# Issue order, piece sizes and the place of an addition in a quantised gated feed-forward kernel: gate casts in halves, gate tiles behind evacuations, two pieces in the first units of down, x1 by VectorE

## The chip, the cores and the metric

One core of one Trainium2 chip. The metric is the device time of one execution in microseconds (us). The engines carry the profile's names: PE (TensorE, matmuls), DVE (VectorE), ACT (ScalarE), POOL (GpSimd) and SP (SyncE, which here issues DMAs). Each engine takes its instructions one after the other in the order in which they were issued to it; an instruction that waits holds up what is behind it on its engine, which the timelines of this kernel show as idle time with a releaser.

## The reference

Two layers on x of 2 x 2048 tokens by 512. The first adds a cross attention to a context of 2 x 128 rows. The second is the one that matters here:

```python
# act_qdq(x): one scale for the whole tensor, x rounded to 16 bit integers
# lpbq_dequant(w): one scale for each block of 32, w rounded to 4 bits
x = act_qdq(x)                                # x: layernorm of layer 1's sum
up = act_qdq(x @ lpbq_dequant(w_up).T)        # 512 -> 1536
gate = act_qdq(x @ lpbq_dequant(w_gate).T)    # 512 -> 1536
sig = fixed_qdq_u16(jax.nn.sigmoid(gate))
gate = act_qdq(gate * sig)
o = act_qdq(gate * up)
return o @ lpbq_dequant(w_down).T             # 1536 -> 512, added to layer 1's sum
```

Each act_qdq needs the maximum over the whole tensor before its first element can be rounded. So the stages gate, up and down follow each other, and what one stage produces is kept or goes through HBM.

## The kernel before

**Exact integers on PE.** The integers of an operand are split into three parts (the integer divided by a base and rounded, in the code `sa`, which ACT casts to part 0; the rest, part 1; and a combination, part 2). A product is then two sums in PSUM: q, over parts 0 and 1, and e, over part 2. ACT *evacuates* q, that is, copies it from PSUM scaled, and DVE then joins e to it.

**Stages** in the profiled execution: attention, layernorm and the weights of gate up to 157 us; gate, 158 to 434; up, 435 to 700; the scale of the product, 700 to 711.5; down, 711.5 to 978.

**Gate** (L683 to L720). Eight token groups of 512, in each three tiles of four chunks: 96 chunks, numbered 0 to 95. A chunk is 12 matmuls (8 for q, 4 for e, 2.72 us on PE). ACT evacuates its q (L712), DVE subtracts e and notes the maximum (L713). q and e have three PSUM buffers each. `split_integers` (L251 to L254) makes the parts of the next token group: sa on DVE, its cast on ACT, parts 1 and 2 on DVE, each over 128 x 2048. Between the chunks a generator advances the preparation of the weights of up and down: eight batches, each with DVE steps over 128 x 1536 (L197 to L213), 12 transposes on PE in three groups (L205, two PSUM buffers) and three copies on ACT (L206).

**Up** (L873 to L900). 48 half tiles c of 24 matmuls (5.44 us). ACT evacuates q (`u`, L876) from two PSUM buffers; DVE subtracts e (L877); ACT takes the absolute value (L817), DVE the maximum of the product with the kept gate values (L818). For each of 24 gate tiles, loaded by SP one and two ahead (`gt`), ACT makes the integers (gi, L769), the sigmoid (L770) and its 16 bit value (sq, L771), each over 128 x 2048; DVE multiplies them to p (L810). `next_gelu` issues the three ACT instructions after a half tile's evacuation in the code, and the scheduler may set them before it. `parts_u` (L750) are the parts of a token group, loaded by SP from HBM.

**The scale of the product** (L905 to L944). While DVE, POOL and ACT find it, PE runs matmuls that nobody reads (`idle`, L912): five behind the transpose of the maxima, one later.

**Down** (L1017 to L1200). 32 units m, one for 128 tokens: 24 matmuls of q (L1032, `yq`) and 12 of e (L1040, `ye`), 8.16 us on PE. A unit's integers o come from p and u: DVE `oi` = p x k_o x u (L1017), DVE `sa` (L1018), ACT cast to part 0 (L1021), DVE part 1 (L1020), DVE part 2 (the "third", L1024). The 1536 inner elements are 12 blocks of 128. Unit 0 takes them in pieces of 2, 2, 4 and 4 blocks, the units 1 to 4 in three pieces of 4, all later ones in one piece of 12. For m = 0 to 3 p is read from the three kept tiles of 4 blocks (`kept_p`); from m = 4 on from one loaded tile (`p5`). The parts have two buffers, by m. ACT also rounds u to integers (`ui`, L995) for the next units.

An output m is finished while unit m + 2 is prepared: ACT evacuates q (`yqs`, L1045), POOL adds x1, which is layer 1's sum (`qx`, L1047), DVE adds the scaled e (L1051) and SP stores it (L1053). The evacuation of m - 2 stands on ACT ahead of the first cast of m. `in_order` (L169) fixes the order in which instructions are issued without a wait; what it does not fix, a scheduler decides.

## Time and profile before

| | us |
|---|---|
| median of 3 runs | 983.13 |
| lowest, highest | 981.88, 984.56 |
| the profiled execution | 983.28 |
| its span in the profile | 981.5 |
| PE busy | 946.1 |
| DVE busy | 816.8 |
| ACT busy | 549.5 |
| POOL busy | 87.1 |

The span begins with the first instruction and ends with the last; the execution's own time is 1.8 us longer. The profile is of one execution. A row of a timeline gives the start, the duration, the engine, the line of the code, the operation, what it writes and reads with shapes, a count when several like rows follow each other, and in brackets how long the engine had stood idle before it and which instruction let it go. Instructions of one engine overlap a little at their ends, so costs that add up are taken from start to start.

### The profile page before, as it was taken

How to read it: one execution, taken by the hardware profiler on the slowest of the kernel's cores; microseconds unless marked ns; L12 is line 12 of the kernel's file. 1: busy time of each engine (PE TensorE's matmuls, PEld its weight loads, DVE VectorE, ACT ScalarE, POOL GpSimd, SP SyncE). 2: the span in 40 equal slices, each digit the busy share in tenths (PEclk: the TensorE clock that was granted, in tenths of full speed). 3: DMA queues.
4: the chain of work that ended last, by engine and by line, in shares of the span. 5: the costliest groups of instructions: out<-in, count | busy, mean ns of one | idle time of the engine just before them, and what ended most of it. 6: DMA issues, size and time to landing. Idle time of an engine off the chain costs nothing. (4 is left out here: it accounts for less than half of the span.)

```text
span 981.5 us, 11779 instructions
## 1 busy us (share of the span) xinstructions
PE 946.1 (96%) x4352; PEld 763.1 (78%) x4352; DVE 816.8 (83%) x1007; ACT 549.5 (56%) x665; POOL 87.1 (9%) x66
## 2 busy tenths in 40 slices
PE   6998889999999999999999999999899999999998
PEld 6775656888878888877888888877587888888886
DVE  4979878898998898447988888969799999998782
ACT  3477699323233323229999999895445355453531
POOL 0101110000000000000000000000111332222221
PEclk9999999999999999999999999999999999999999
DMA  9675546976995954896997979979783686656710
GB/s 358 244 283 200 186 166 262 410 303 243 383 359 182 344 195 170 282 410 244 373 323 290 406 284 368 379 264 407 294 326 117 222 268 234 203 177 227 263 62 36
DMA packets 103596, 263.72 MB, mean 269 GB/s; under 512 B 6064, under 2 KB 46000, under 8 KB 94832
## 3 DMA queue, kind: packets, MB, share of 16 engines
q1 hardware_dynamic: 102496, 259.02, 71.4%
q0 software_dynamic: 512, 2.88, 0.8%
q10 hardware_dynamic: 528, 1.05, 0.3%
q8 instruction: 34, 0.56, 0.2%
q14 instruction: 26, 0.21, 0.1%
HBM read 136.05 MB, written 126.88 MB: 268 GB/s over the span
## 5 line engine op out<-in xcount | busy, mean ns | idle before, releaser
L621 PE MATMUL q_g<-parts_g,wg 128*128 128x512 f32 x768 | 192.7, 392 | 2.1 <-ACT g L712 1.2
L621 PEld LDWEIGHTS q_g<-parts_g,wg 128*128 128x128 f32 x768 | 143.1, 188 | 32.6 <-ACT parts_g L644 2.0
L712 ACT ACTIVATE g<-q_g 128x512 f32<-128x512 f32 x96 | 57.2, 599 | 168.3 <-PE q_g L621 157.6
L621 PE MATMUL q_u<-parts_u,wu 128*128 128x512 f32 x576 | 142.5, 389 | 1.8 <-ACT u L876 1.2
L621 PEld LDWEIGHTS q_u<-parts_u,wu 128*128 128x128 f32 x576 | 108.0, 188 | 24.9 <-ACT u L876 2.6
L1032 PE MATMUL yq<-wd,o_parts 128*128 128x512 f32 x512 | 121.6, 389 | 0.5 <-ACT o_parts L1021 0.5
L1032 PEld LDWEIGHTS yq<-wd,o_parts 128*128 128x128 f32 x512 | 96.0, 188 | 21.0 <-ACT o_parts L1021 0.9
L627 PE MATMUL e_g<-parts_g,wg 128*128 128x512 f32 x384 | 103.3, 390 | 0.0
L713 DVE CUSTOM_DVE_ANT_0 g<-g,e_g 128x512 f32<-128x512 f32 x96 | 64.4, 679 | 40.1 <-PE e_g L627 36.8
L1021 ACT CAST o_parts<-sa 128x1536 fp32r<-128x1536 int16 (+2 forms) x43 | 49.1, 1145 | 67.9 <-DVE sa L1018 67.7
L627 PEld LDWEIGHTS e_g<-parts_g,wg 128*128 128x128 f32 x384 | 71.8, 188 | 15.2 <-DVE gtop L713 0.3
L1047 POOL TENSOR_TENSOR qx<-yqs,x 128x512 f32<-128x512 f32 x32 | 63.1, 1973 | 205.2 <-ACT yqs L1045 147.0
L627 PE MATMUL e_u<-parts_u,wu 128*128 128x512 f32 x288 | 77.0, 389 | 0.0
L1024 DVE SCALAR_TENSOR_TENSOR o_parts<-sa,oi 128x1536 fp32r<-128x1536 int16 (+2 forms) x43 | 62.5, 1475 | 10.9 <-PE ye L1040 10.9
L877 DVE TENSOR_TENSOR u<-u,e_u 128x1024 f32<-128x1024 f32 x47 | 56.8, 1217 | 16.6 <-ACT u L876 16.5
L1032 PE MATMUL yq<-first_wd,o_parts 128*128 128x512 f32 x256 | 65.2, 398 | 3.7 <-ACTq L1090 2.1
L1045 ACT ACTIVATE yqs<-yq,q_o 128x512 f32<-128x512 f32 x32 | 21.9, 684 | 80.3 <-PE yq L1032 80.2
L818 DVE CUSTOM_DVE_ANT_0 ua<-ua,pi 128x1024 f32<-128x1024 f32 x46 | 56.0, 1219 | 12.9 <-ACT ua L817 12.8
L1020 DVE SCALAR_TENSOR_TENSOR o_parts<-sa,oi 128x1536 fp32r<-128x1536 int16 (+2 forms) x43 | 59.0, 1372 | 8.3 <-PE yq L1032 5.3
L1040 PE MATMUL ye<-wd,o_parts 128*128 128x512 f32 x256 | 63.2, 389 | 0.0
L627 PEld LDWEIGHTS e_u<-parts_u,wu 128*128 128x128 f32 x288 | 54.1, 188 | 11.2
L1032 PEld LDWEIGHTS yq<-first_wd,o_parts 128*128 128x128 f32 x256 | 48.9, 192 | 15.7 <-ACTq L1090 2.9
(213 smaller groups left out, 1571.6 us busy)
## 6 DMA issues: line engine op xcount, KB each, us to landing
gate_d<-g SPq DMA_DIRECT2D x24, 1024.0 KB, 7.7
up_d<-u SPq DMA_DIRECT2D x48, 512.0 KB, 8.8
gt<-gate_d SPq DMA_DIRECT2D x22, 1024.0 KB, 8.3
u<-up_d SPq DMA_DIRECT2D x21, 1024.0 KB, 9.0
parts_d<-parts_g SPq DMA_DIRECT2D x6, 3072.0 KB, 12.3
parts_u<-parts_d SPq DMA_DIRECT2D x6, 3072.0 KB, 15.6
p_d<-pi SPq DMA_DIRECT2D x24, 512.0 KB, 9.9
p<-p_d SPq DMA_DIRECT2D x84, 128.0 KB, 2.8
```

Of the source, the lines that this page charges most:

```text
L621: nc.tensor.matmul(q, lhsT=w[:, s, c, :], rhs=parts[:, s, c, :], start=(c + s == 0), stop=(c + s == ND))
L627: made = nc.tensor.matmul(e, lhsT=w[:, 2, c, :], rhs=parts[:, 2, c, :], start=(c == 0), stop=(c == ND - 1))
L712: evacuated = nc.scalar.activation(g4[:, i, :], q, AF.Copy, scale=1.0 + 1.0 / BASE)
L713: subtracted = nc.vector.tensor_tensor_reduce(g4[:, i, :], g4[:, i, :], e, 1.0, LOWEST, ALU.subtract, ALU.max, gtop[:, m : m + 1])
L818: nc.vector.tensor_tensor_reduce(ua, ua, pi, 1.0, 0.0, ALU.mult, ALU.max, pumax[:, c : c + 1])
L877: less = nc.vector.tensor_tensor(u4[:, both, :], u4[:, both, :], e, ALU.subtract)
L1020: made.append(nc.vector.scalar_tensor_tensor(parts[1][:, c], sa[:, c], -BASE, oi[:, c], ALU.mult, ALU.add))
L1021: return made, nc.scalar.copy(parts[0][:, c], sa[:, c])
L1024: return nc.vector.scalar_tensor_tensor(parts[2][:, c], sa[:, c], BASE + 1.0, oi[:, c], ALU.mult, ALU.subtract)
L1032: nc.tensor.matmul(q, lhsT=parts[s][:, f, :], rhs=wd[f][:, s, :], start=(f + s == 0), stop=(f + s == NF))
L1040: nc.tensor.matmul(e, lhsT=parts[2][:, f, :], rhs=wd[f][:, 2, :], start=(f == 0), stop=(f == NF - 1))
L1047: nc.gpsimd.tensor_tensor(qx, qs, x1[:, m % NU, :], ALU.add)
```

## The change

Four edits, in the order of the diff.

1. Gate: from token group 1 on, `split_integers` works in two halves of 128 x 1024 (sa, cast, parts 1 and 2 of the first half, then of the second). The scheduler then orders much of gate's DVE and ACT work anew.
2. Up: from half tile 4 on, the first of the three ACT instructions of a gate tile may not be issued ahead of the evacuation of that half tile.
3. The scale of the product: six and two idle matmuls for five and one.
4. Down: the units 1 to 4 take their blocks in two pieces, 4 and 8; in the units 1 to 3 the piece of 8 reads p with two instructions of 4, since p lies in two tiles. Part 2 is one instruction of 12 (in unit 0, one of 4 and one of 8). The outputs 0 to 3 have no POOL addition: ACT evacuates to `qs`, DVE adds the scaled e into it and then adds x1 in an instruction of its own, and the store reads `qs`, which has two buffers. In unit 0 the small operations of the output's scale stand behind part 2. The three round-ups of u that are issued with unit 3 stood one behind each cast; now one stands behind the first cast and two behind the second.

```diff
@@ -683,7 +683,7 @@
                 if t == 0:
                     parts = first
                 else:
-                    parts = split_integers(wk1, homes[t % 2], hi[t], [ND, TG], f"g{t}")
+                    parts = split_integers(wk1, homes[t % 2], hi[t], [ND, TG], f"g{t}", 2)
                 if t < NG - 2:
                     nc.sync.dma_start(out=parts_d[t], in_=parts.bitcast(F32))
                 else:
@@ -762,11 +762,13 @@
         s_g16 = const.tile([P, 1], F32, name="s_g16")
         nc.vector.tensor_scalar(s_g16, s_g, 1.0 / 65536.0, None, ALU.mult)
 
-        def gelu_like(pool, gt, shape, name):
+        def gelu_like(pool, gt, shape, name, behind=None):
 
             sq = pool.tile([P] + shape, U16, tag="sq", name=f"sq_{name}")
             gi = pool.tile([P] + shape, I16, tag="gi", name=f"gi_{name}")
-            nc.scalar.activation(gi, gt, AF.Copy, scale=r_g)
+            begun = nc.scalar.activation(gi, gt, AF.Copy, scale=r_g)
+            if behind is not None:
+                in_order(behind, begun)
             nc.scalar.activation(gt, gi, AF.Sigmoid, scale=s_g)
             nc.scalar.activation(sq, gt, AF.Copy, scale=65536.0)
             return gi, sq
@@ -792,11 +794,11 @@
 
         wd, ready, made_p = [], [], []
 
-        def next_gelu():
+        def next_gelu(behind):
 
             j = len(ready)
             if j < len(order):
-                ready.append(gelu_like(wk3, gts.pop(0), [NQ, TG], j))
+                ready.append(gelu_like(wk3, gts.pop(0), [NQ, TG], j, behind))
                 if j + 2 < len(order):
                     gts.append(load_gate(j + 2))
 
@@ -873,7 +875,7 @@
                     e = ps_m.tile([P, 2, TG], F32, tag="e", name=f"e_u{c}")
                     for i in range(2):
                         project(wu2[i], parts, q[:, i, :], e[:, i, :])
-                    nc.scalar.activation(u4[:, both, :], q, AF.Copy, scale=1.0 + 1.0 / BASE)
+                    evacuated = nc.scalar.activation(u4[:, both, :], q, AF.Copy, scale=1.0 + 1.0 / BASE)
                     less = nc.vector.tensor_tensor(u4[:, both, :], u4[:, both, :], e, ALU.subtract)
                     if c + 2 == NH:
                         in_order(row_known, less)
@@ -890,7 +892,8 @@
                     load_down(range(NE, NE + NQ), slice(0, 2))
                 stored = nc.sync.dma_start(out=up_d[c], in_=u4[:, both, :])
                 if h == 0 or c in more_gelu:
-                    next_gelu()
+
+                    next_gelu(evacuated if c > 3 else None)
                 if h == 0 or c in more_p:
                     next_p()
                 pi = kept_p[j % NK]
@@ -918,7 +921,7 @@
 
 
         a_u, turned = over_partitions_by_pe(ps_m, "q", [P, 2, TG], umax, "u")
-        in_order(before[-1], turned, *(behind := idle(5, u4[:, 0, :])))
+        in_order(before[-1], turned, *(behind := idle(6, u4[:, 0, :])))
 
         r_u = const.tile([P, 1], F32, name="r_u")
         nc.vector.tensor_scalar(r_u, a_u, 1.0 / QMAX, tiny_u, ALU.mult, ALU.max)
@@ -939,7 +942,7 @@
             if i == 0:
                 nc.vector.tensor_scalar(most[:, 3:4], best[:, 1:2], r_u, 1.0 + 2.0**-18, ALU.mult, ALU.mult)
                 nc.vector.tensor_scalar(most[:, 3:4], most[:, 3:4], 0.5 * (QMAX + 2.0), None, ALU.add)
-        in_order(behind[-1], *idle(1, product[:, :TG]))
+        in_order(behind[-1], *idle(2, product[:, :TG]))
         top = const.tile([P, 4], F32, name="top")
         nc.gpsimd.partition_all_reduce(top, most, P, bass_isa.ReduceOp.max)
 
@@ -1011,10 +1014,15 @@
         ]
         oi, sa = (wki.tile([P, NF, P], I16, tag=tag, bufs=1, name=tag) for tag in ("oi", "sa"))
 
-        def round_o(parts, pi, ui, c=slice(None)):
-
+        def round_o(parts, pis, ui, c=slice(0, NF)):
+
+            n = (c.stop - c.start) // len(pis)
             made = [
-                nc.vector.scalar_tensor_tensor(oi[:, c], pi, k_o, ui, ALU.mult, ALU.mult),
+                nc.vector.scalar_tensor_tensor(
+                    oi[:, ds(c.start + i * n, n)], pi, k_o, ui[:, ts(i, n)], ALU.mult, ALU.mult
+                )
+                for i, pi in enumerate(pis)
+            ] + [
                 nc.vector.tensor_scalar(sa[:, c], oi[:, c], 1.0 / BASE, None, ALU.mult),
             ]
             made.append(nc.vector.scalar_tensor_tensor(parts[1][:, c], sa[:, c], -BASE, oi[:, c], ALU.mult, ALU.add))
@@ -1043,6 +1051,8 @@
         def finish_first(m, q, x1):
             qs = wk2.tile([P, D], F32, tag="qs", name=f"yqs_{m}")
             made = nc.scalar.activation(qs, q, AF.Copy, scale=q_o)
+            if m < NS * NU:
+                return made, qs
             qx = wk2.tile([P, D], F32, tag="qx", name=f"qx_{m}")
             nc.gpsimd.tensor_tensor(qx, qs, x1[:, m % NU, :], ALU.add)
             return made, qx
@@ -1050,6 +1060,9 @@
         def finish(m, qx, e):
             made = nc.vector.scalar_tensor_tensor(qx, e, e_o, qx, ALU.mult, ALU.add)
             t = m // NU
+            if m < NS * NU:
+
+                nc.vector.tensor_tensor(qx, qx, x1s[t][:, m % NU, :], ALU.add)
             nc.sync.dma_start(out=of[ds(groups[t // NS] * TG + t % NS * TD + m % NU * P, P), :], in_=qx)
             return made
 
@@ -1068,10 +1081,11 @@
             nc.vector.reciprocal(k_o, k_o)
 
         def scale_of_o():
-            nc.vector.tensor_tensor(s_o, a_o, s_pu, ALU.mult)
+            begun = nc.vector.tensor_tensor(s_o, a_o, s_pu, ALU.mult)
             nc.vector.tensor_scalar(s_o, s_o, 1.0 / QMAX, TINY, ALU.mult, ALU.max)
             nc.vector.tensor_scalar(q_o, s_o, BASE + 1.0, None, ALU.mult)
             nc.vector.tensor_scalar(e_o, s_o, -BASE, None, ALU.mult)
+            return begun
 
         uis = {0: up_integers(0)}
         a_o = const.tile([P, 1], F32, name="a_o")
@@ -1084,7 +1098,7 @@
         factor_of_o()
 
 
-        first_made, first_cast = round_o(o_parts[0], kept_p[0][:, :2, :P], uis[0][:, :2, :P], slice(0, 2))
+        first_made, first_cast = round_o(o_parts[0], [kept_p[0][:, :2, :P]], uis[0][:, :2, :P], slice(0, 2))
         in_order(*first_made)
         known = nc.values_load(flag[0:1, 0:1], min_val=0, max_val=1)
         with tc.If(known == 0):
@@ -1136,7 +1150,7 @@
                     nc.vector.tensor_copy(kept_p[k], pv)
                 scale_of_pu()
                 factor_of_o()
-                in_order(*round_o(o_parts[0], kept_p[0][:, :2, :P], uis[0][:, :2, :P], slice(0, 2))[0])
+                in_order(*round_o(o_parts[0], [kept_p[0][:, :2, :P]], uis[0][:, :2, :P], slice(0, 2))[0])
 
         ld = c5.enter_context(tc.tile_pool(name="ld", bufs=2))
         last = NT // TD - 1
@@ -1156,43 +1170,41 @@
                 if j == NU - 1 and t < last:
                     x1s[t + 1] = load_x1(t + 1)
                 ui, w, parts = uis[t], ts(j, P), o_parts[m % 2]
-                if t < NS or m == NS * NU:
-
-                    casts, made = [], []
-                    sizes = [2, 2, NQ, NQ] if m == 0 else [NQ] * NK
-                    pieces = [slice(sum(sizes[:i]), sum(sizes[: i + 1])) for i in range(len(sizes))]
-                    for n, c in enumerate(pieces):
-                        if m == n == 0:
-                            continue
+
+                sizes = {0: [2, 2, NQ, NQ], NS * NU: [NQ, 2 * NQ]}.get(m, [NQ, 2 * NQ] if t < NS else [NF])
+                pieces = [slice(sum(sizes[:i]), sum(sizes[: i + 1])) for i in range(len(sizes))]
+                casts, made = [], []
+                for n, c in enumerate(pieces):
+                    if m == n == 0:
+                        continue
+                    if t < NS:
                         k, i = divmod(c.start, NQ)
-                        if t < NS:
-                            v = kept_p[k][:, ds(i, c.stop - c.start), ds(t * TD + j * P, P)]
+                        at = ds(t * TD + j * P, P)
+                        if c.stop - c.start > NQ:
+                            v = [kept_p[k + d][:, :, at] for d in range((c.stop - c.start) // NQ)]
                         else:
-                            v = p5[t][:, c, w]
-                        done, cast = round_o(parts, v, ui[:, c, w], c)
-                        made += done
-                        casts.append(cast)
-                    made += [third_part(parts, c) for c in pieces]
-                    in_order(*made)
+                            v = [kept_p[k][:, ds(i, c.stop - c.start), at]]
+                    else:
+                        v = [p5[t][:, c, w]]
+                    done, cast = round_o(parts, v, ui[:, c, w], c)
+                    made += done
+                    casts.append(cast)
+                if m == 0:
+                    made += [third_part(parts, slice(0, NQ)), third_part(parts, slice(NQ, NF))]
                 else:
-                    made, cast = round_o(parts, p5[t][:, :, w], ui[:, :, w])
-                    casts = [cast]
                     made.append(third_part(parts))
-                    in_order(*made)
+                in_order(*made)
                 if m > 1:
                     in_order(evacuated, casts[0])
                 sums[m] = first_sum(m, parts), second_sum(m, parts)
                 if m == 0:
-                    scale_of_o()
+                    in_order(made[-1], scale_of_o())
                     in_order(casts[-1], *round_up(ui, 0, P, P))
                 if j == (0 if t == 0 else NU - 1) and t < last:
                     uis[t + 1] = up_integers(t + 1)
                     rounded = round_up(uis[t + 1], t + 1)
                     if t == NS - 1:
-                        for cast, done in zip(casts, rounded):
-                            in_order(cast, done)
-                        in_order(rounded[0], casts[1])
-                        in_order(rounded[1], casts[2])
+                        in_order(casts[0], rounded[0], casts[1], *rounded[1:])
                     else:
                         in_order(casts[-1], *rounded)
                     if t % NS == NS - 2 and t + NS <= last:
```

## The prediction

> **What bounds the kernel now.** The page's first section gives PE 96% of the span, so only PE's waits can be won. I read the table of PE's waits first, for those near the edited lines; then the timelines of the engines that end them; then the order in which the changed program issues its instructions on each engine. Four are near the edits (columns: engine, line, who released it: us in total, times, longest):

> ```profile
> PE q_u L621 <- ACT u L876: 2.6, 2, 1.3
> PE yq L1032 <- ACT o_parts L1021: 2.2, 2, 1.6
> PE yq L1032 <- ACTq L1090: 2.1, 1, 2.1
> ...
> PE q_g L621 <- ACT g L712: 1.2, 1, 1.2
> ```

> With smaller ones PE idles 12.9 us after 150 us. That is all there is to win behind the preparation.

> **Down's first units.** The timeline from 743 to 757 shows what L1032 waits for. First PE, then DVE, then POOL (start, duration, what it does, in brackets idle time and releaser):

> ```profile
> 750.43 2.11 PE L1032 MATMUL yq<-wd,o_parts 128*128 128x512 f32 x8 [0.53 <-ACT o_parts L1021]
> ...
> 756.89 0.50 PE L1032 MATMUL yq<-first_wd,o_parts 128*128 128x512 f32 x1 [1.64 <-ACT o_parts L1021]
> ```

> ```profile
> 747.57 0.75 DVE L1017 SCALAR_TENSOR_TENSOR oi<-p,k_o,ui 128x512 int16<-128x512 int16 x1
> 748.35 1.32 DVE L1018 TENSOR_SCALAR sa<-oi 128x512 int16<-128x512 int16 x1
> 749.78 0.69 DVE L1020 SCALAR_TENSOR_TENSOR o_parts<-sa,oi 128x512 fp32r<-128x512 int16 x1
> 750.39 1.89 DVE L1024 SCALAR_TENSOR_TENSOR o_parts<-sa,oi 128x512 fp32r<-128x512 int16 x3
> 752.20 0.74 DVE L1051 SCALAR_TENSOR_TENSOR qx<-ye,e_o,qx 128x512 f32<-128x512 f32 x1
> 752.86 1.81 DVE L1017 SCALAR_TENSOR_TENSOR oi<-p,k_o,ui 128x1536 int16<-128x1536 int16 x1
> 754.77 0.56 DVE L1018 TENSOR_SCALAR sa<-oi 128x1536 int16<-128x1536 int16 x1
> ```

> ```profile
> 748.23 1.29 POOL L1047 TENSOR_TENSOR qx<-yqs,x 128x512 f32<-128x512 f32 x1 [6.57 <-ACT yqs L1045]
> ```

> DVE has no idle time from 711.4 to 757: here it is the bound, and PE follows it through the cast. The sa row of 1.32 us begins while POOL's add runs; the same shape takes 0.29 at 719 to 747 us where POOL is quiet. The four adds of outputs 0 to 3 meet sa at 728.59 (1.19) and 748.35 (1.32) and the thirds at 722.97 (2.98) and 740.42 (3.00, against 1.89): 0.90 + 1.03 + 1.09 + 1.11 = 4.1 us of DVE.

> What one unit costs on DVE: a 4-wide piece is oi, sa, p1, start to start 0.78 + 0.33 + 0.61 = 1.72 (up to 1.8 further on), three of them 5.3; thirds 1.81; finish 0.66; in all 7.8, and with an add 8.9. PE's unit is 8.16 (729.79 to 737.96).

> After: a 4-wide piece stays 1.72. The 8-wide one has two oi (0.66 + 0.78), one sa and one p1 over 1024, which the trace lacks: by the 512 and the 1536 rows sa lies from 0.33 to 0.67, p1 from 0.61 to 1.76 (start to start); I take the middles, 0.50 and 1.19, since 1024 lies in the middle: piece 3.13. The third over 1536 is 1.76. Sum 6.61. A finish is 0.66 plus the new add of x1, taken as 0.61 (512-wide rows start 0.60 to 0.66 apart); x1 lies there, since POOL reads it at these times now. Unit: 7.88, with nothing on POOL until m = 4's add. So DVE falls under PE's 8.16.

> Walk: m = 0 is unchanged up to 715.95, its thirds end 717.75. m = 1 is done at 724.4, m = 2 at 731.0, finish 0 at 732.2, m = 3 at 738.9, finish 1 at 740.1, m = 4 at 746.7, finish 2 at 748.0. Then m = 5 as before: from oi's start to PE's start 756.89 - 752.86 = 4.03, so 752.0. PE needs it at 729.79 + 3 x 8.16 = 754.3, or 2.3 us later. PE's start of m = 1 at 721.50 stays: it is set by ACT, whose cast at 720.84 stands behind six round-ups of 5.07 us. **Gain: 756.89 - 754.27 = 2.6 us**; with sa and p1 at their upper ends, 0.74 more in each of four units, 3.0 in all, the slack goes and 0.7 with it: 1.9. More than 2.6 is not to be had, since PE then is the bound. The idle time of 0.53 + 1.64, with overlap lost at both, says the same.

> What is new: the outputs 0 to 3 are stored from qs, two buffers, so the evacuation of y2 waits for the store of y0, y3's for y1's. Behind it on ACT stand the first cast of m = 4 and of m = 5. Stores land after 2.0 us (median 2.8, one of 11.1). Finish 0 ends at 732.2; with 0.3 for the issue, y2's buffer is free at 734.5 to 743.6, and m = 4's cast is due at 745.5. For y3: 742.4 to 751.5, its evacuation of 0.68, and m = 5's cast of 1.47 has to start at 752.8. I cost it at nothing; were each store the slowest, 0.6 us of cover would be left. The 3 DMA issues of these outputs on SP come no later than before.

> [...]

> **Idle matmuls**, one more at two places. One takes 0.43 per pass, 0.86 in all (L912: 10 passes, 4.46). They fill PE gaps of 1.28 (ends 708.35) and 2.08 (ends 711.55), whose ends other engines set: 707.93 and 710.4 are earlier. Cost 0; if they ran at half clock, 0.3. The granted clock is 0.5 from 711.29 to 714.70, so that down's first 8 matmuls take 3.55 instead of 1.98. If busier PE avoids this, PE waits for m = 1's cast at 721.5 all the same: gain 0 to 0.2, and 1.0 if ACT's round-ups were not last. I take 0.

> **Gate.** PE's stall at 270.5 is read from ACT:

> ```profile
> 268.29 1.91 ACT L252 CAST parts_g<-sa_g 128x2048 fp32r<-128x2048 int16 x1 [7.13 <-DVE sa_g L251]
> 270.11 1.06 ACT L206 COPY wsp_u<-wt_u 128x512 f32<-128x512 f32 x2
> 271.43 0.58 ACT L206 COPY wsp_u<-wt_u 128x512 f32<-128x512 f32 x1 [0.26 <-PE wt_u L205]
> 271.91 1.59 ACT L712 ACTIVATE g<-q_g 128x512 f32<-128x512 f32 x3
> ```

> ACT stood 7.13 us at a cast whose sa DVE made late (267.54, behind weight steps and a maximum); three evacuations queued behind it, and PE lost 0.24 + 1.17 us and its overlap, some 0.16. In the changed order the halves of this sa stand on DVE behind chunk 33's subtraction, and the casts on ACT behind evacuation 35, with the weight's transposes later: the cast finds its input ready, the stall of 1.6 goes. What is late next: the transposes of a weight batch, which use two PSUM buffers; adding row by row, six of the eight batches have their third group wait 0.23, against two such waits before (0.24 in that stall, 0.26 at 354.6). Net 1.2, bounds 0 and 1.6.

> Price of the halves: start to start 2.21 over 2048 and 0.61 over 512 give 1.14 over 1024, so 0.08 more for each of 3 x 7 operations, 1.6 us of DVE and as little on ACT (1.91 against two of 1.0). DVE is 105 of 113 us busy in this stage and runs behind PE by up to two chunks, which three PSUM buffers cover. One spot is tight: the second half of token group 2's third part stands behind chunk 23's subtraction and is needed 2.3 us after chunk 24 begins (10 matmuls of 0.227); subtraction 0.69 and half 1.14 leave 0.4. If DVE is a weight step late there (1.75), PE waits 1.3.

> [...]

> **Up.** The gelu tile's gi moves behind the evacuation. Up to evacuation 9 ACT's order is the same, so the 1.34 at 462.70 stays. The other 1.23 is at the end:

> ```profile
> 658.44 2.00 ACT L769 ACTIVATE gi<-gt,r_g 128x2048 int16<-128x2048 f32 x1 [0.24 <-DMA gt<-gate_d]
> 660.35 1.00 ACT L876 ACTIVATE u<-q_u 128x1024 f32<-128x1024 f32 x1
> 661.26 2.00 ACT L770 ACTIVATE gt<-gi,s_g 128x2048 f32<-128x2048 int16 x1
> ```

> After, gate tile 20's gi starts 2.8 us earlier (633.0), but evacuations 36 to 39 now stand behind the sigmoid, 1.9 later in the order. Walk: u36 637.8, u37 645.3, u38 653.8 to 655.0, u39 ends 661.4 to 662.6 (before 661.26), the spread from the load of the next gate tile, which SP issues when the tile two back is done and which lands 7.2 to 8.8 us later. Cost -0.1 to +1.3. But the same load, moved 2.7 us up, lets SP issue the load of parts_u earlier, and PE's 0.52 us wait for it at 667 goes. Net -0.5 to +0.8; I take 0.

> **Sum.** 2.6 + 0 + 1.2 + 0 = 3.8 off the profiled execution's 983.28 (span 981.5 and 1.8 around it; 0.15 over the median of three, 983.13): **979.4 us**.

> **Rivals.** What a measurement can tell from no change is about 0.3%, 2.95 us, so "faster" means under 980.2.
> - *Forecast*, 0.48: 978.3 to 980.6; under 980.2 in 0.42 of it.
> - *Down's gain alone*, 0.27: gate's tight spot (1.3) and up's tail (0.8) take back what gate gives: 983.28 - 2.6 - 1.2 + 2.1 = 981.6; with either, 980.3 to 981.0. For it: DVE at 93% in gate.
> - *More*, 0.13: all of gate's 1.6, up's 0.5, and up to 1.0 from the clock: 983.28 - 2.6 - 3.1 = 977.6, down to 976.5.
> - *Down doesn't do what it says*, 0.06: the long sa and thirds came from the loads and stores of these units and not from POOL, and stay: 4.1 later, and half of the 3.0 above: 757.6, no gain but 0.7 lost; with gate 983.28 + 0.7 - 1.2 = 982.8. Against: all four stand beside an add.
> - *Slower*, 0.06: in gate DVE falls a whole weight step behind at each of the six boundaries between token groups 1 to 7, so a half comes 1.2 late at each: +7.2 - 2.6 = 987.9. At group 2 it decides from a DVE backlog of 0.4; against it: at the other boundaries the halves stand three or more chunks of 2.72 ahead, and a backlog of 8 us would be needed.

> So faster 0.42 + 0.13 = 0.55, same 0.06 + 0.27 + 0.06 = 0.39, slower 0.06. The range 976.5 to 983.0 leaves out the last case and the noise of the runs (981.88 to 984.56) above it.

> **What would show it.** Down: PE without a wait on L1021, m = 5 at 754.3 less the earlier gains; sa never over 0.6. Gate: no wait of PE for g L712, its end 1.2 earlier. Up: 1.3 at evacuation 3 as before, and 1.2 to 2.5 near half tile 41. Wrong would be PE waiting for casts of the gate, stores that hold up yqs, or a stall that moves from L1021 to L1045.

## The result, and the profile after

The changed kernel takes 980.62 us, the median of 20 executions (978.43 to 984.71), against 983.58 for 20 of the kernel before (980.76 to 985.75): a ratio on record of 0.9975, with a 95% interval of 0.9966 to 0.9984 (the two medians alone give 0.9970). That is a gain of 0.25%, clear of noise and less than the 0.4% of the forecast. The profiled execution of the changed kernel took 981.48, its span is 979.7.

The two spans differ by 1.8 us only, and they may not be compared as they stand. Cut by PE's own marks, which are the first matmul of each stage:

| stretch (us) | before | after | difference | forecast |
|---|---|---|---|---|
| start to gate's first q_g | 158.29 | 159.49 | +1.20 | 0 |
| gate, to up's first q_u | 276.92 | 275.38 | -1.54 | -1.2 |
| up, to the transposes of the maxima | 267.27 | 268.01 | +0.74 | 0 |
| scale, to unit 0 of down | 9.07 | 9.07 | 0 | 0 |
| down, unit 0 to unit 5 | 45.34 | 43.07 | -2.27 | -2.6 |
| unit 5 to the end | 224.60 | 224.69 | +0.09 | 0 |

The first row has nothing to do with the change. The granted clock shows 0.5 for one window of 3.413 us in the preparation before, and for two after. Over all 14 profiled executions of this study the first q_g came at 156.5 to 156.8 in four without such a window, at 158.2 to 158.6 in seven with one in the profile's records of that stretch, and at 158.2 to 159.9 in three with two. Single executions of one kernel lie 5 to 6 us apart, and these windows go with some 3 of it (the first q_g at 156.5 to 159.9). Without that row the change is worth 2.98 us in this pair of profiles, inside the interval of the timed runs (0.9966 to 0.9984 of 983.6 is 1.6 to 3.3 us). So the stretches are the finer measure, and the experiments are read by them.

The table of PE's waits after, cut to the lines that answer to those of before (in L621 the line of ACT is now L878, in down L1029 stands for L1021, L1104 for L1090):

```profile
PE q_u L621 <- ACT u L878: 3.5, 3, 1.7
...
PE yq L1040 <- ACT o_parts L1029: 1.2, 3, 0.5
...
PE yq L1040 <- ACTq L1104: 1.2, 1, 1.2
```

Gate's wait for g is gone from the table. Up has three waits and 3.5 us where it had two and 2.6. Down still waits for casts, but three times for little: these are in the units 0 and 1, and none is in unit 4 or 5. PE's timeline after, at unit 5, shows no idle time where there were 1.64 us:

```profile
753.20 1.98 PE L1048 MATMUL ye<-wd,o_parts 128*128 128x512 f32 x8
755.02 1.98 PE L1040 MATMUL yq<-first_wd,o_parts 128*128 128x512 f32 x8
```

DVE's timeline after, for one unit (m = 3), which is to be read against the unit of before:

```profile
733.79 0.29 DVE L1026 TENSOR_SCALAR sa<-oi 128x512 int16<-128x512 int16 x1
734.19 0.69 DVE L1028 SCALAR_TENSOR_TENSOR o_parts<-sa,oi 128x512 fp32r<-128x512 int16 x1
734.80 1.41 DVE L1021 SCALAR_TENSOR_TENSOR oi<-pi,k_o,ui 128x512 int16<-128x512 int16 x2
736.31 0.43 DVE L1026 TENSOR_SCALAR sa<-oi 128x1024 int16<-128x1024 int16 x1
736.85 1.22 DVE L1028 SCALAR_TENSOR_TENSOR o_parts<-sa,oi 128x1024 fp32r<-128x1024 int16 x1
738.00 1.75 DVE L1032 SCALAR_TENSOR_TENSOR o_parts<-sa,oi 128x1536 fp32r<-128x1536 int16 x1
739.66 0.75 DVE L1061 SCALAR_TENSOR_TENSOR yqs<-ye,e_o,yqs 128x512 f32<-128x512 f32 x1
```

From start to start: sa over 1024 costs 0.54 here (forecast 0.50), p1 1.15 (1.19), part 2 over 1536 1.66 (1.76), and no sa is stretched.

And ACT's timeline after, around gate's old stall:

```profile
261.70 0.60 ACT L712 ACTIVATE g<-q_g 128x512 f32<-128x512 f32 x1 [2.12 <-PE q_g L621]
262.60 2.00 ACT L252 CAST parts_g<-sa_g 128x1024 fp32r<-128x1024 int16 x2 [0.31 <-PE e_g L627]
264.51 0.59 ACT L712 ACTIVATE g<-q_g 128x512 f32<-128x512 f32 x1
267.14 0.60 ACT L712 ACTIVATE g<-q_g 128x512 f32<-128x512 f32 x1 [2.04 <-PE q_g L621]
```

The cast no longer waits 7 us for sa, and PE waits for no evacuation of gate any more.

### The profile page after: what moved, and what is told of

It reads as the page before. It is cut to its first block, busy times and chain, and to the rows that moved or that the text cites. A ratio compares the mean times of both kernels' runs of the same rounds, so it can differ in the third digit from the quotient of the medians.

```text
span 979.7 us, 11777 instructions
## 1 busy us (share of the span) xinstructions
PE 947.5 (97%) x4356; PEld 763.4 (78%) x4356; DVE 812.5 (83%) x1013; ACT 548.7 (56%) x668; POOL 77.9 (8%) x62
## 5 line engine op out<-in xcount | busy, mean ns | idle before, releaser
L621 PE MATMUL q_g<-parts_g,wg 128*128 128x512 f32 x768 | 193.1, 391 | 0.9 <-ACT parts_g L644 0.9
L621 PEld LDWEIGHTS q_g<-parts_g,wg 128*128 128x128 f32 x768 | 143.4, 188 | 31.2 <-ACT parts_g L644 2.0
L712 ACT ACTIVATE g<-q_g 128x512 f32<-128x512 f32 x96 | 57.3, 598 | 166.0 <-PE q_g L621 155.5
L621 PE MATMUL q_u<-parts_u,wu 128*128 128x512 f32 x576 | 142.7, 390 | 2.6 <-ACT u L878 2.6
L621 PEld LDWEIGHTS q_u<-parts_u,wu 128*128 128x128 f32 x576 | 107.9, 188 | 26.1 <-ACT u L878 3.7
L1029 ACT CAST o_parts<-sa 128x1536 fp32r<-128x1536 int16 (+3 forms) x39 | 48.4, 1243 | 44.5 <-DVE sa L1026 44.3
L1032 DVE SCALAR_TENSOR_TENSOR o_parts<-sa,oi 128x1536 fp32r<-128x1536 int16 (+2 forms) x33 | 60.0, 1819 | 14.8 <-PE ye L1048 14.8
L1057 POOL TENSOR_TENSOR qx<-yqs,x 128x512 f32<-128x512 f32 x28 | 54.0, 1928 | 211.8 <-ACT yqs L1053 140.9
L1028 DVE SCALAR_TENSOR_TENSOR o_parts<-sa,oi 128x1536 fp32r<-128x1536 int16 (+3 forms) x39 | 57.4, 1472 | 9.7 <-PE yq L1040 7.0
L878 ACT ACTIVATE u<-q_u 128x1024 f32<-128x1024 f32 x47 | 47.7, 1014 | 23.4 <-PE q_u L621 23.2
```

The lines of the kernel that those rows point to most:

```text
L621: nc.tensor.matmul(q, lhsT=w[:, s, c, :], rhs=parts[:, s, c, :], start=(c + s == 0), stop=(c + s == ND))
L712: evacuated = nc.scalar.activation(g4[:, i, :], q, AF.Copy, scale=1.0 + 1.0 / BASE)
L1028: made.append(nc.vector.scalar_tensor_tensor(parts[1][:, c], sa[:, c], -BASE, oi[:, c], ALU.mult, ALU.add))
L1029: return made, nc.scalar.copy(parts[0][:, c], sa[:, c])
L1032: return nc.vector.scalar_tensor_tensor(parts[2][:, c], sa[:, c], BASE + 1.0, oi[:, c], ALU.mult, ALU.subtract)
L1057: nc.gpsimd.tensor_tensor(qx, qs, x1[:, m % NU, :], ALU.add)
```

## The experiments

Each run is the changed kernel with the edit that is shown. "Unit 1" and "unit 5" are the starts of these units after unit 0's. Of the start of the span nothing is compared, for the reason above.

| run | gate | up | scale | unit 1 | unit 5 | ratio to before, interval |
|---|---|---|---|---|---|---|
| before | 276.92 | 267.27 | 9.07 | 9.94 | 45.34 | |
| after | 275.38 | 268.01 | 9.07 | 10.30 | 43.07 | 0.9975, 0.9966 to 0.9984 |
| up_undone | 275.37 | 269.07 | 9.07 | 10.29 | 43.08 | 0.9953, 0.9936 to 0.9969 |
| up_undone_again | 275.33 | 268.30 | 9.07 | 10.30 | 43.09 | |
| gate_undone | 277.17 | 267.89 | 9.07 | 9.95 | 42.73 | 0.9980, 0.9967 to 0.9994 |
| gate_order | 276.62 | 267.82 | 9.07 | 9.95 | 42.72 | 0.9987, 0.9973 to 1.0000 |
| gate_copy_later | 276.99 | 267.84 | 9.07 | 9.95 | 42.72 | |
| idles_undone | 275.30 | 269.85 | 9.07 | 10.44 | 43.09 | 0.9970, 0.9957 to 0.9982 |
| pool_adds | 275.33 | 268.27 | 9.08 | 10.29 | 43.07 | |
| three_pieces | 275.35 | 268.65 | 9.07 | 10.29 | 43.07 | |
| up_both | 275.25 | 266.68 | 9.07 | 10.29 | 43.08 | 0.9955, 0.9939 to 0.9971 |
| up_tail | 275.39 | 266.39 | 9.08 | 10.29 | 43.07 | 0.9948, 0.9934 to 0.9961 |
| up_tail_shift | 275.32 | 265.96 | 9.08 | 10.30 | 43.09 | 0.9950, 0.9937 to 0.9964 |
| gate_undone_shift | 277.03 | 267.85 | 9.08 | 10.30 | 43.08 | |

Gate repeats to 0.15 us between the runs that leave it as it is, and scale and down to 0.02, so differences of 0.3 in them mean something. Up repeats to 0.3 to 0.9 only; why is told below. The intervals of the timed runs overlap among most of the variants.

### Down: the additions alone, the pieces alone

`pool_adds` gives the addition of x1 for the outputs 0 to 3 back to POOL and keeps the pieces:

```diff
         made = nc.scalar.activation(qs, q, AF.Copy, scale=q_o)
-            if m < NS * NU:
-                return made, qs
...
-            if m < NS * NU:
-
-                nc.vector.tensor_tensor(qx, qx, x1s[t][:, m % NU, :], ALU.add)
```

> The changed kernel in which POOL adds x1 to the outputs 0 to 3 again; the two pieces stay. From unit 0's first matmul to unit 5's first the changed kernel took 43.07 us, the kernel before 45.34. In the changed kernel unit 5's cast was done 2.7 us before PE wanted it. Theory A (both parts of the edit shorten DVE, and either alone is almost enough): four adds stretch DVE's work by 4 x 1.0 and take away four additions of 0.61, 1.7 in all, less than 2.7: 43.1 to 43.4. Theory B (the gain is POOL's, the pieces bring little): 44 or more. The long rows of sa and the thirds, of 1.0 more, come back in either.

`three_pieces` keeps the additions on DVE and has three pieces and three thirds in the units 1 to 4:

```diff
-                sizes = {0: [2, 2, NQ, NQ], NS * NU: [NQ, 2 * NQ]}.get(m, [NQ, 2 * NQ] if t < NS else [NF])
+                sizes = {0: [2, 2, NQ, NQ], NS * NU: [NQ] * NK}.get(m, [NQ] * NK if t < NS else [NF])
...
+                elif len(pieces) > 1:
+                    made += [third_part(parts, c) for c in pieces]
```

> The changed kernel with three pieces of 4 and three thirds in the units 1 to 4, as before; DVE adds x1 as in the change. Unit 0's first matmul to unit 5's first: 43.07 in the changed kernel, 45.34 before. Theory A (either alone is almost enough): three pieces cost 0.5 to 0.6 a unit more, 2.2 in four, less than the 2.7 of slack: 43.1 to 43.5, with every sa at 0.3. Theory B (the gain is the pieces', the additions bring little): 44 or more.

Both came out at 43.07, as the changed kernel. What differs is how early unit 5's cast is done (its end on ACT against PE's start of unit 5): 2.7 us in the changed kernel, 0.9 with POOL's additions, 0.26 with three pieces. So POOL's additions cost 1.8 and the third piece 2.4 (2.2 was expected). For the additions 1.7 was expected, but its own terms, 4 x 1.0 less 4 x 0.61, make 1.6, and the rows come to 1.8 by another way. Ahead of unit 5's cast four operations were lengthened by 0.8, 0.9, 1.0 and 0.4, in all 3.1; three additions went from DVE and not four, and each had put off the sa behind it by 0.41 to 0.48 only, in all 1.3. Two rows of DVE in `pool_adds`, and two of POOL's additions there, show the same stretch as before the change; the third group, of `three_pieces`, shows it absent:

```profile
726.90 1.33 DVE L1026 TENSOR_SCALAR sa<-oi 128x1024 int16<-128x1024 int16 x1
...
739.99 1.26 DVE L1026 TENSOR_SCALAR sa<-oi 128x512 int16<-128x512 int16 x1
```

```profile
726.35 1.60 POOL L1055 TENSOR_TENSOR qx<-yqs,x 128x512 f32<-128x512 f32 x1 [2.62 <-ACT yqs L1053]
739.45 1.65 POOL L1055 TENSOR_TENSOR qx<-yqs,x 128x512 f32<-128x512 f32 x1 [11.50 <-ACT yqs L1053]
```

```profile
727.89 0.29 DVE L1026 TENSOR_SCALAR sa<-oi 128x512 int16<-128x512 int16 x1
...
744.75 0.29 DVE L1026 TENSOR_SCALAR sa<-oi 128x512 int16<-128x512 int16 x1
```

Theory A holds: either edit alone lifts DVE over PE's pace and wins all that is to be won; the second one buys slack. That POOL's additions stretch DVE is shown by `pool_adds` and the changed kernel, which differ in the place of the addition alone: sa takes 1.33 over 1024 and 1.26 over 512 there, against 0.43 and 0.29 in the unit of the changed kernel above. So the rival that put the long rows down to loads and stores falls.

### Gate: whole casts again

`gate_undone` has `split_integers` in one piece:

```diff
-                    parts = split_integers(wk1, homes[t % 2], hi[t], [ND, TG], f"g{t}", 2)
+                    parts = split_integers(wk1, homes[t % 2], hi[t], [ND, TG], f"g{t}")
```

> The changed kernel with part 1 undone: the casts of gate in one piece. Gate, from PE's first q_g to its first q_u, took 276.91 before and 275.39 after. Theory (the stall behind the late cast of token group 4 comes back whole): 276.9 with PE's waits of 0.24 and 1.17 near 270. Rival (part of the 1.5 comes from elsewhere in the stage): under 276.5. PE's first wait of up, which was 1.34 before and 0.85 after: back to 1.34 if gate's order moved it, either value if it is a matter of one execution.

Gate is back at 277.17, with PE's waits of 0.26 and 1.18, as the theory had it:

```profile
272.39 0.66 PE L205 MATMUL wt_u<-ident,w_u 128*128 128x128 f32 x4 [0.26 <-ACT wsp_u L206]
274.22 2.11 PE L621 MATMUL q_g<-parts_g,wg 128*128 128x512 f32 x8 [1.18 <-ACT g L712]
```

Up's first wait stayed at 0.85, so gate's order does not make it.

`gate_order` then asks whether it was the length of the casts or only the order. It is `gate_undone` with one swap on DVE:

```diff
+            divided = nc.vector.tensor_scalar(a[:, c], n[:, c], 1.0 / BASE, None, ALU.mult)
+            if name == "g4":
+                in_order(divided, tops[8])
...
+                    tops.append(abs_max(gmax[:, n : n + 1], g4, AX.XY))
```

> The changed kernel with the casts of gate in one piece, and one change of order: the division (sa) of token group 4 on DVE stands ahead of the maximum of gate tile 8, which takes 2.2 us, and not behind it. Theory (what counted was how late that sa was, not the length of a cast): ACT's cast starts 2.2 earlier, the 1.4 of waits near 270 go, gate 275.3 to 275.5. Rival (halves are needed, since a whole cast of 1.9 holds up the evacuations wherever it stands): 276 or more.

276.62: the theory missed. The cast began 2.2 us earlier, as meant, but PE's 1.18 stayed. ACT's timeline shows why:

```profile
266.06 1.91 ACT L256 CAST parts_g<-sa_g 128x2048 fp32r<-128x2048 int16 x1 [4.88 <-DVE sa_g L253]
267.87 1.06 ACT L206 COPY wsp_u<-wt_u 128x512 f32<-128x512 f32 x2
270.98 0.59 ACT L206 COPY wsp_u<-wt_u 128x512 f32<-128x512 f32 x1 [2.04 <-PE wt_u L205]
271.46 1.59 ACT L716 ACTIVATE g<-q_g 128x512 f32<-128x512 f32 x3
```

The third copy waits 2.04 us for PE, whose third group of transposes comes after chunk 38, and the evacuations 36 to 38 stand behind that copy. PE then waits for evacuation 36. So behind the late sa there lay a second reason of the same length.

`gate_copy_later` takes that away too; the third copy goes behind evacuation 38:

```diff
+            copied[name, b] = nc.scalar.copy(ws[:, 2, b, :], pt)
...
+                        if m == 38:
+                            in_order(evacuated, copied["u3", 2])
```

> As the run gate_order (one cast, its sa ahead of the maximum), and ACT's third copy of the weight batch stands behind evacuation 38 and not ahead of evacuation 36. Gate took 277.17 with the whole cast, 276.62 with the sa ahead, 275.38 with the halves. Theory (what is left is a chain by order alone: evacuation 36 behind the third copy, the third copy behind PE's third group of transposes, which PE takes after chunk 38, and chunk 39 behind evacuation 36): no wait for g at 271, 275.3 to 275.6. Rival (a whole cast holds up the evacuations): the wait of 1.18 stays and gate is 276.4 or more.

276.99, and the theory missed again. The wait for g is gone, and another of 1.35 us has come in its place, on the other PSUM tile of the same chunk. PE first, then DVE, of this run:

```profile
270.98 2.12 PE L625 MATMUL q_g<-parts_g,wg 128*128 128x512 f32 x8
274.45 1.19 PE L631 MATMUL e_g<-parts_g,wg 128*128 128x512 f32 x4 [1.35 <-DVE gtop L719]
```

```profile
265.95 2.29 DVE L180 TENSOR_REDUCE gmax<-g 128x1 f32<-128x2048 f32 x1
268.15 2.29 DVE L257 SCALAR_TENSOR_TENSOR parts_g<-sa_g,hi 128x2048 fp32r<-128x2048 int16 x1
270.35 2.29 DVE L258 SCALAR_TENSOR_TENSOR parts_g<-sa_g,hi 128x2048 fp32r<-128x2048 int16 x1
273.10 0.69 DVE L253 TENSOR_SCALAR sa_g<-hi 128x2048 int16<-128x2048 int16 x1 [0.46 <-DVE parts_g L258]
273.71 0.68 DVE L719 CUSTOM_DVE_ANT_0 g<-g,e_g 128x512 f32<-128x512 f32 x1
```

Three steps of 2.2 us stand in a row on DVE, then the sa of the token group after, with an idle 0.46 ahead of it, and the subtractions that give e's PSUM back come after them. So the old stall had three reasons, each of 1.2 to 1.4 us, one behind the other: the late sa, the copy ahead of the evacuations, the long steps ahead of the subtractions. One swap of order wins 0.55 of 277.17, and both together 0.18, since the next reason takes over each time. The halves, with the order that the scheduler made of them, are free of all three. My theory that order alone would do it was not borne out for the two swaps tried; whether a third, between DVE's long steps, would close it was not tried, and neither were halves in the old order. So it is not shown how much of the 1.8 between `gate_undone` and the changed kernel is due to the halves themselves and how much to the new order that came with them.

### Up: the old order, twice

`up_undone` lets a gate tile's first instruction stand ahead of the evacuation again:

```diff
-                    next_gelu(evacuated if c > 3 else None)
+                    next_gelu(None)
```

> The changed kernel with part 2 undone: a gate tile's first ACT instruction may again stand ahead of the evacuation. The up stage, from PE's first q_u to the transposes of the maxima, took 267.27 us before and 268.01 after. Theory (the new place costs at the end of up: ACT's order there puts evacuations 36 to 39 behind the sigmoid): up back to 267.3, with waits of 1.2 on L876 near half tile 41 and 0.5 on parts_u; the total 0.7 less than the changed kernel. Rival (the longer tail comes from the landing of the gate tile's load, by chance of that one execution): up stays at 268.0.

Up was 269.07, and not 267.3: neither theory said that the old order would be the slower. ACT's order at the end was that of before. What differed is the last gate tile's load, which landed later:

```profile
656.94 2.00 ACT L769 ACTIVATE gi<-gt,r_g 128x2048 int16<-128x2048 f32 x1 [1.48 <-DMA gt<-gate_d]
658.84 1.00 ACT L878 ACTIVATE u<-q_u 128x1024 f32<-128x1024 f32 x1
```

> The run up_undone once more, for a second execution with the old order in up. Its up took 267.27 in the kernel before and 269.07 in up_undone, where gate tile 23 waited 0.24 and 1.48 for its load. Theory (with the old order, the end of up hangs on when that load lands): up between 267 and 269.2, and the higher the longer that wait. Rival (the halves in gate or something else of the change costs the 1.8): 269.0 whatever the wait.

`up_undone_again` is the same kernel, executed once more. It gave 268.30, with a wait of 0.72 for the load. With the old order up was 267.27, 268.30 and 269.07, at waits of 0.24, 0.72 and 1.48: in the order of the waits, as the theory says. The tail alone shows it better: from half tile 35's first matmul to the transposes it took 75.11, 75.56 and 76.32, which is 74.84 to 74.87 and the wait for the load. Why the load lands later in some executions stays open.

With the new order and no half clock in it, up was 267.8 to 268.7 in seven executions, always with the same two waits of PE at the end, 0.93 and 1.64 to 1.69, and a tail of 75.99 to 76.00. In the changed kernel ACT's evacuation 36 (the last row) stands behind a gate tile's first instruction, a pause and a sigmoid. PE's two waits of before, of after, and ACT of after:

```profile
661.41 2.11 PE L621 MATMUL q_u<-parts_u,wu 128*128 128x512 f32 x8 [1.23 <-ACT u L876]
...
667.66 2.32 PE L621 MATMUL q_u<-parts_u,wu 128*128 128x512 f32 x9 [0.52 <-DMA parts_u<-parts_d]
```

```profile
655.18 2.34 PE L621 MATMUL q_u<-parts_u,wu 128*128 128x512 f32 x9 [0.93 <-ACT u L878]
...
662.62 2.11 PE L621 MATMUL q_u<-parts_u,wu 128*128 128x512 f32 x8 [1.68 <-ACT u L878]
```

```profile
632.54 1.99 ACT L769 ACTIVATE gi<-gt,r_g 128x2048 int16<-128x2048 f32 x1
636.37 1.06 ACT L819 ACTIVATE ua<-u 128x1024 f32<-128x1024 f32 x1 [1.84 <-DVE u L879]
637.34 2.00 ACT L772 ACTIVATE gt<-gi,s_g 128x2048 f32<-128x2048 int16 x1
639.24 1.00 ACT L878 ACTIVATE u<-q_u 128x1024 f32<-128x1024 f32 x1
```

So the edit of up trades a tail that hangs on one load for a tail that is always the same, and it does not gain by it. From half tile 6, which lies behind up's first wait, to the transposes the old order took 232.87, 233.31 and 234.08, on average 233.42, and the new one 233.89 to 234.09 in the seven executions, on average 233.93: 0.5 more. The timed runs point the same way, 0.9953 for `up_undone` against 0.9975 for the changed kernel, though the two intervals overlap a little and `up_undone` has four runs.

The other part of up's spread is its first wait, behind evacuation 3. It was 0.85 where DVE found POOL's maximum a_g ready, 1.18 where DVE waited 0.36 for it, and 1.51 where it waited 0.86 or 1.10. Before, DVE waited 0.53 and PE 1.34. The 1.51 came with either order of up. The 0.85 came in six executions, all with the new order, but ACT's order up to evacuation 3 is the same in both, and only three executions have the old one; why POOL's result comes later in some executions stays open.

### Up's end mended

The timeline of after shows ACT idle for 0.90, 0.34 and 2.06 us between 625 and 632, ahead of gate tile 20's first instruction, which stands behind evacuation 35, and then with no pause from 636.4 to 666. `up_both` puts that instruction ahead of evacuation 35 (the list's first entry is not a gate tile, so 21 is gate tile 20), and evacuation 3 ahead of a sigmoid:

```diff
+            begins.append((begun, nc.scalar.activation(gt, gi, AF.Sigmoid, scale=s_g)))
...
+                    if c == 35:
+                        in_order(begins[21][0], evacuated)
+                    if c == 3:
+                        in_order(evacuated, begins[3][1])
```

> The changed kernel with two more constraints on ACT's order in up: evacuation 3 ahead of the sigmoid of gate tile 2, and the first instruction of gate tile 20 ahead of evacuation 35 and not behind it. Up took 268.01 in the changed kernel, with PE waits of 0.85 behind evacuation 3, and 0.93 and 1.68 behind the evacuations 38 and 39. Theory (ACT's order alone makes these waits: it stood idle 627 to 636 while gate tile 20 was there, and then had no pause to 668): all three go, with 0.16 of lost overlap each, up 264.2 to 264.8, the whole some 3.5 us less. Rival (gate tiles 20 to 23 come as late as their loads, which SP issues when a buffer is free): tile 20 waits for its load, evacuation 35 behind it, and PE; up 266 or more.

266.68, which is 1.3 less than after, little more than a third of what was expected. The theory missed, and the rival had the number (266 or more), though not the place: gate tile 20 did not wait for its load, an earlier gate tile did. The first wait went, and PE, 1.0 earlier now, waited 1.48 us at 537 behind an evacuation that stood behind that gate tile:

```profile
525.60 2.00 ACT L771 ACTIVATE gi<-gt,r_g 128x2048 int16<-128x2048 f32 x1 [2.22 <-DMA gt<-gate_d]
```

`up_tail` has the first of the two constraints alone (`begins` is made as in `up_both`):

```diff
+                    if c == 35:
+                        in_order(begins[21][0], evacuated)
```

> The changed kernel with one more constraint on ACT: the first instruction of gate tile 20 stands ahead of evacuation 35 and not behind it. Up took 268.0 to 268.7 in six executions of kernels with the changed order (0.85 to 1.5 of it behind evacuation 3), and 266.68 with this constraint and a second one that moved evacuation 3; there a wait of 1.48 near 537 took back what the second one had won. Theory (the constraint alone takes off the end of up what it took off there, and the wait near 537 came from PE running ahead of a late gate tile): the waits behind the evacuations 38 and 39, 2.6 together, shrink to under 1.0, none near 537, up 266.0 to 266.9. Rival (PE has to wait once for the gate tiles anyway, as their loads set it): a new wait elsewhere, up over 267.5.

266.39, with nothing at 537 and 0.73 at 648 in place of 0.93 and 1.68, as the theory had it. The tail from half tile 35 on is 73.92, against 76.00 with the changed order and 75.11 at best with the old one. Timed, it is 0.9948 of the kernel before (0.9934 to 0.9961; median 978.42, five executions), the lowest number of this study, which the timed runs do not tell from `up_tail_shift`, `up_undone` and `up_both` (0.9950 to 0.9955). It carries the whole change and one line of order more. Against the changed kernel it takes 0.9973 of the time, by the ratios of the two to the kernel before; an interval for that pair was not measured, and the two intervals just fail to overlap.

### Idle matmuls

`idles_undone` has five and one of them again:

```diff
-        in_order(before[-1], turned, *(behind := idle(6, u4[:, 0, :])))
+        in_order(before[-1], turned, *(behind := idle(5, u4[:, 0, :])))
...
-        in_order(behind[-1], *idle(2, product[:, :TG]))
+        in_order(behind[-1], *idle(1, product[:, :TG]))
```

> The changed kernel with five and one idle matmuls again. Scale stage, from the transposes of the maxima to the first yq: 9.07 before and after. Theory (they fill time that others set): 9.07 again, and unit 1 starts 10.0 to 10.3 after unit 0, set by ACT, whether or not the granted clock falls. Rival A (they keep the clock up, and that is worth time): a window of half clock in 711 to 716, unit 0's first 8 matmuls 3.5 instead of 2.4, and unit 1 later by up to 1. Rival B (they delay the branch: DVE stood 0.89 at it after and 0.54 before): 0.54 again, unit 1 0.35 earlier.

The scale stage stayed at 9.07. The half-clock window came back at 712.2 to 715.6, where the kernel before has one, and none of the twelve executions with six and two does. Four matmuls took 2.04 instead of 1.20 in it, and unit 1 started 0.14 later; ACT's round-ups cover the rest. At unit 5 0.02 of it was left. So rival A is right about the clock and wrong about its worth. (Its up, 269.85, has another such window, at 661.0 to 664.4.) Rival B fell: DVE's time at the branch stayed.

### The branch ahead of down

In the changed kernel unit 1 starts 0.35 later after unit 0 than before. DVE comes out of the branch at L1104 that much later, first before, then after:

```profile
711.40 0.48 DVE L1017 SCALAR_TENSOR_TENSOR oi<-pi,k_o,ui 128x256 int16<-128x256 int16 x1 [0.54 <-DVEq L1090]
```

```profile
712.14 0.49 DVE L1021 SCALAR_TENSOR_TENSOR oi<-pi,k_o,ui 128x256 int16<-128x256 int16 x1 [0.89 <-DVEq L1104]
```

It went with the halves in gate, which have nothing to do with the branch but put 21 more DVE records ahead of it (a record is an instruction or a wait of DVE in the trace). It takes back a part of what the halves win: `gate_undone` loses 1.79 in gate and gains 0.34 at unit 5. `gate_undone_shift` is `gate_undone` with 21 instructions that write a tile that nobody reads:

```diff
-    ctx.enter_context(tc.tile_pool(name="fill", bufs=1)).tile([P, 48], F32, name="fill")
+    fill = ctx.enter_context(tc.tile_pool(name="fill", bufs=1)).tile([P, 48], F32, name="fill")
+    for i in range(21):
+        nc.vector.memset(fill[:, i : i + 1], 0.0)
```

> The run gate_undone (whole casts in gate, 998 DVE records ahead of the branch, the next one 0.16 after it, unit 1 9.95 after unit 0) with 21 more DVE instructions of one element a row at the program's start, so 1019 records as in the changed kernel. Theory (the number of DVE instructions ahead of the branch, and with it the place of the code behind it, sets the 0.16 or 0.50): 0.50, and unit 1 10.3 after unit 0. Rival (the halves of gate do it by something else): 0.16 and 9.95.

With 21 more, DVE's next record came 0.52 after the branch, not 0.16, and unit 1 at 10.30, not 9.95: more instructions ahead of the branch do it without the halves.

> As the run up_tail, with 16 more DVE instructions of one element a row at the program's start, which write a tile that nobody reads. In all four executions in which 998 or 1000 DVE records lie ahead of the branch, DVE's next record came 0.16 after it, and in all six with 1019 to 1021 it came 0.50 after it; unit 1 started 9.94 and 10.29 after unit 0. Theory (how DVE's code lies in memory sets how soon it is there after the branch): with 1035 it is either of the two, and another value or 0.16 would show that the place of the code decides. Rival (it comes from what the halves of gate do to the engine's state or to the DMA queues): 0.50 again, as the halves stay. Nothing else changes.

`up_tail_shift` adds 16 of them, by the same edit, to `up_tail`; with 1036 records it stayed at 0.51, so that run told nothing apart by itself. In all: 0.16 at 998 and 1000 records, 0.50 to 0.52 at 1019 to 1036. The runs show that the time after the branch goes with the count; whether the place of the code is behind it, as the theories have it, is not shown.

## Why the prediction was right or wrong

The forecast was 979.4 for the profiled execution, faster by 3.8. It was right in its direction and its range (976.5 to 983.0), and too high in its gain: by a quarter against the 2.98 of the stretches, by half against the 2.5 us that 0.25% make. By the line that it drew itself, faster under 980.2, the median of 980.62 counts as the same, to which it gave 0.39 against 0.55. By its steps:

- **Down's DVE as the bound, 2.6.** Right, to 0.05: from unit 1 to unit 5 it took 35.40 us (45.34 - 9.94) before and 32.77 (43.07 - 10.30) after. The sizes held too: a unit of the walk was 6.61, and m = 2's took 6.73 (725.14 to 731.87). In part two slips cancel there: the walk took 1.76 over 1536 as a time from start to start, which is a duration (from start to start part 1 is 1.68, 755.44 to 757.12 before), and its 4-wide piece of 1.72 was 1.86 in that unit. The cast of m = 5 was ready 2.7 us early, forecast 2.3.
- **What the two edits of down share.** The prediction added their savings and noted that PE, at 8.16 a unit, is the bound then. It did not say that one of them is enough. The two experiments show it.
- **The new wait for stores.** It came: the evacuation of y3 waited 0.94 us for a store, and the cast behind it was not late. Cost nothing, as taken.

```profile
746.42 0.69 ACT L1053 ACTIVATE yqs<-yq,q_o 128x512 f32<-128x512 f32 x1 [0.94 <-DMA out<-yqs]
750.84 1.48 ACT L1029 CAST o_parts<-sa 128x1536 fp32r<-128x1536 int16 x1 [3.73 <-DVE sa L1026]
```

- **Unit 1's start at 9.95 after unit 0, "unchanged".** The step that failed in down: 0.35 later, since DVE left the branch later. No row of the profile before could have shown it: only the runs told that it goes with the count of records ahead of the branch (0.16 at 998 and 1000, 0.50 to 0.52 at 1019 to 1036).
- **Idle matmuls, 0.** Right, and the clock window went as the prediction allowed, for 0.14 at unit 1 and 0.02 at unit 5.
- **Gate, 1.2.** The mechanism was right for the changed order: the stall went. The term mis-sized is the six waits of 0.23 for the weights' PSUM; five of 0.05 came, so the gain was 1.54. The sum was also wrong: the stall of 1.6 and the old wait of 0.26, less six waits of 0.23, make 0.5 and not 1.2, so that 1.2 came as near as it did by luck. The tight spot at token group 2 did not wait. What the prediction had too simple is the stall's cause: it named the late sa, and two more reasons lay behind it.
- **Up, 0.** It came out at +0.74, at the end of the range given (-0.5 to +0.8), and that it lies inside is luck: behind the first wait up took 1.22 longer (232.87 and 234.09; 0.88 of it in the tail from half tile 35 on, the rest in small gaps ahead of it), and the first wait, forecast to stay 1.34, came out 0.49 shorter for POOL's reasons and not for the edit's. The walk was right in kind: the evacuations behind the sigmoid cost more, the wait for parts_u went. The term mis-sized is the tail: 0.93 + 1.68 where 1.23 + 0.52 stood. It was mis-sized since the walk let gate tile 20 begin right after evacuation 35, and then its sigmoid and evacuation 36 follow; in the run ACT stood 1.84 us at the absolute value in between, which waited for DVE. The 1.22 holds for this pair of profiles; against the three executions of the old order the loss is 0.5 on average.

So of the rivals "Down's gain alone" was nearest: its 981.6 lies by the profiled 981.48 only because of the 1.20 of the preparation, but its case of one of two losses, 980.3 to 981.0, holds the median of 980.62. Of its two losses gate's tight spot did not come and up's tail did; gate gave all it could, and up and the branch took 1.1 back.

## What to carry to other kernels

When a stall is traced to a late instruction, list what else stands behind it on each engine that serves the waiting one: here a copy and a run of long steps were as late, and removing one won 0.55 us of 1.8, removing two 0.18. Two edits that relieve the same bound do not add once the next engine's pace is reached, so measure each alone and read the slack, not the time. A wait that varies by itself can hide what an edit costs behind it in the same stage, so cut the stage at that wait. Compare stages by the engine that sets them, not whole spans, where windows of half clock went with a start that lay up to 3.4 us apart (the first q_g at 156.5 to 159.9).
